# Graph-network kernel on one core: 64-wide products laid in pairs on the two column halves of TensorE, and the first message round reordered

## The chip, the cores and the metric

The kernel runs on one NeuronCore of a Trainium2 chip. The metric is the device time of one execution in microseconds (us). Three runs of the kernel before took 3177.02 to 3182.76 us, with a median of 3179.41 us. The engines are named as in the profile: PE is TensorE's matmul side and PEld its weight loads, DVE is VectorE, ACT is ScalarE, POOL is GpSimd, and SP issues transfers.

## The reference

Sixteen graphs (batches) of 1024 nodes with 64 channels go through four layers. `x` is [16, 1024, 64], `adj` is [16, 1024, 1024] with about 1.6% of its entries and its diagonal not zero, all in float32. Cut to what matters:

```python
x = layernorm(x + (adj @ (x @ W0) + b0))                      # layer 0
a = drop(adj)              # two neighbours of a row with over 10 of them are dropped, in both directions
agg = 0.25*q25(x, a) + 0.5*q50(x, a) + 0.25*q75(x, a)         # quantiles over a node's neighbours, per channel
x = layernorm(x + relu((x + agg) @ W1 + b1) @ W2 + b2)        # layer 1 (times the node mask)
h = x @ We
for i in range(3):
    h = relu(adj @ (h @ Wl[i] + bl[i]))
x = layernorm(x + (h @ Wp + bp))                              # layer 2 (times the node mask)
t = adj @ x
x = layernorm(x + where(t > 0.5, 1, 0))                       # layer 3
```

## The kernel before, in words

The nodes of a graph are 8 tiles (`T`) of 128. `adj` is transposed on TensorE, block by block, since its products need it with the source node on the partitions. Every batch goes through these parts, each written as a Python generator:

- `words_of` (with `transposed` and `Layer0`): rows of `adj` are loaded (`load_row`, L417, two buffers), transposed (L439) and copied out by ScalarE (L441). DVE tests the entries (`nb`, L526), TensorE packs the tests into words (L536). `Layer0.feed` (L464) multiplies the transposed tile with x: for every tile eight products with a weight of 128 rows by 64 columns and 128 moving columns, summed over the eight source tiles into partitions 0 to 63 of a PSUM bank. `Layer0.end` transposes x itself into the lower 64 partitions of `ax` (L478, copies L480), and one product per tile with W0 stacked on an identity (L485) gives adj x W0 plus x, with the bias. A layernorm gives x1.
- `front` and `listing`: the words become lists of neighbours, mostly on DVE (L646 one-hot rows, L694 to L710 list steps), with products that permute rows (L651, L652). Their last product for the table, L575, must be done before the table of x1 rows is written to DRAM.
- `gathered`: POOL gathers neighbour rows by indirect transfers (L815) into one of four sort buffers. `masked`: ScalarE adds a mask to each gathered row (L868). `quantiles`: DVE runs sorting networks of minimum and maximum over the rows (L906), in five groups of tiles per batch. `summed`: ScalarE weighs the sorted rows (L932), TensorE adds them with an identity (L936), and ScalarE or DVE copies the sums.
- `back`: `to_nodes` brings the aggregates into node order, with one-hot rows `ones_at` (L974 and L975 on ScalarE; in the last batch two of three on DVE, L971) and products of three bfloat16 pieces (L979), adds x1 (L985) and copies two halves to `oT` (L988). Then come the W1 product (L1172), `residual` with W2 (L1141, and L1147 and L1149 on DVE), layernorm to x2; `to_channels` transposes x2 (L367, copies L369); the embedding (L1185, copies L1187); three rounds, each with a message (bias L324, products L1196, copies L1199) and an aggregation over the whole of `adj` (L1207, 128 by 128 weights with 512 moving columns, relu L1210); the projection (L1141), layernorm to x3; `aggregate` for layer 3 (L377, 128 by 64 weights, 512 moving columns, copies L380), transposition back (L1219), the comparison on DVE (L1222), and the last layernorm. Layernorm's lines are L390 to L411, with ScalarE's square at L396 and DVE's last product at L411.

`adj` transposed is kept in DRAM per batch (`adjd`) and loaded whole (4 MB) into one buffer `adjB` for `back`.

The order of the work on each engine is written by the end of the function: every part has a planned start on a common clock, and a queue takes the part with the least time next. A part's `yield 1.3` says how long its last step is planned to take, times a stretch per part (`WORDS / WORDS_STEPS`, `BACK / BACK_STEPS` and so on). The five groups have planned lengths of 192 us together, which is the planned period of a batch:

```python
LENGTHS = (50.06, 35, 54.5, 19.5, 33)
...
            add(start(q), quantiles(st, g), (start(q + 1) - start(q)) / (cost + 0.1))
```

No time is measured: each engine runs its instructions in the order so written, and waits for their inputs. The setup before it (constants, weights, biases, the node mask) is ordered by dependencies; `centred` takes the mean over channels out of weights and biases that feed a layernorm, and `bias16` holds the biases in three bfloat16 pieces, added by a product with ones (`add_bias`, L324).

In f32 one product is two matmul instructions, each with its own weight load. At the end `general` stands for batches in which the lists run over; its branch is not taken here.

Of the kernel before, what the change touches and what calls it, by code (L numbers as in the profile page):

```python
# [10 lines left out]
F32 = mybir.dt.float32  # L11
# [142 lines left out]
def kernel(  # L154
# [126 lines left out]
    nc.scalar.dma_start(w0_sb[:C, :], w0)  # L281
    nc.vector.tensor_copy(w0_sb[C:, :], ident[C:, C:])
    w1_sb = load("w1_sb", [C, H], w1)
    b1_sb = load("b1_sb", [H, 1], b1.unsqueeze(1))
    w2_sb = load("w2_sb", [H, C], w2)
    we_sb = load("we_sb", [C, H], we)
# [11 lines left out]
    for v, n in ((w0_sb, 2 * C), (w2_sb, H), (wp_sb, H)):  # L298
        centred(v, n)
# [21 lines left out]

    def add_bias(bank, first, n, times):

        nc.tensor.matmul(bank[:, :times * n], ones16,  # L324
                         bias16[:, first:first + n].unsqueeze(1).to_broadcast([S, times, n]),
                         start=True, stop=False)
# [4 lines left out]
    mask_f = const.tile([B * T, P], F32, name="mask_f")  # L331
# [29 lines left out]

    def to_channels(dst, src):

        for h in range(NH):
            pt = psum_mm()
            for i in range(TH):
                nc.tensor.transpose(pt[:C, i * P:(i + 1) * P], src[:, h * TH + i, :], ident)  # L367
            yield 1.5
            nc.scalar.copy(dst[:, h * HALF:(h + 1) * HALF], pt[:C, :])  # L369
            yield 1.0  # L370

    def aggregate(dst, adjT, src, bank):

        for h in range(NH):
            pa = bank()
            for m in range(T):
                nc.tensor.matmul(pa[:C, :], src[:, m, :], adjT[:, h * TH:(h + 1) * TH, m, :],  # L377
                                 start=(m == 0), stop=(m == T - 1))
                yield 1.3
            nc.scalar.copy(dst[:, h * HALF:(h + 1) * HALF], pa[:C, :])  # L380
            yield 0.7
# [38 lines left out]
    def load_x(b):  # L420
        xt = act.tile([P, T + 1, C], F32, tag="x", name="xt")
        nc.vector.memset(xt[:, 0, :], 0.0)
        nc.sync.dma_start(xt[:, 1:, :], one(x, b).rearrange("o (t p) c -> p (o t) c", p=P))
# [28 lines left out]
    class Layer0:  # L452
# [6 lines left out]
        def feed(self, t, at):  # L459
# [3 lines left out]
            for m in range(T):  # L463
                nc.tensor.matmul(self.bank[:C, cols], self.xt[:, m + 1, :], at[:, m, :],  # L464
                                 start=(m == 0), stop=(m == T - 1))
            yield 2.4
            if t % TH == TH - 1:
                h = t // TH
                nc.scalar.copy(self.ax[:C, h * HALF:(h + 1) * HALF], self.bank[:C, :])
                yield 0.7  # L470

        def end(self, y):
            for h in range(NH):
                pt = psum_tp()
                for i in range(TH):

# [839 lines left out]
```

## Time and profile before

| What | us |
|---|---|
| Median of three runs | 3179.41 |
| Profiled execution: its span, the only time the page gives of it | 4328.2 |
| DVE busy in it | 2822.0 (65%) |
| PE busy | 2647.8 (61%) |
| PEld busy | 1635.7 (38%) |
| POOL busy | 2160.8 (50%) |
| ACT busy | 1914.0 (44%) |
| First and last sort step on DVE (L906) | from 266.8 to 4195.2 |
| Mean granted TensorE clock | 0.764 |

The profiled execution is 1149 us longer than the median of the runs. Shares of the span are therefore not shares of a timed run, while busy times of single instructions can be carried over. The largest groups on TensorE are L1207 (769.6 us in 1536 instructions), L936 (376.0 us), L464 (284.5 us in 1920), L377 (272.6 us in 512) and L979 (213.0 us in 768). DVE's largest groups are the forms of L906. A mean duration on PE mixes two clocks: the granted clock moves between half and full speed.

### The profile page before, as it was taken

Reading aid. Unit: us, or ns where it says so; the run is one execution under the profiler, and the core shown is the slowest. Engines: PE = TensorE matmul, PEld = TensorE weight load, DVE = VectorE, ACT = ScalarE, POOL = GpSimd, SP = SyncE. Lnnn points to the kernel's source line nnn. Section 1 sums busy time; section 2 is a strip of 40 time slices with the busy share of each in tenths; the row PEclk is TensorE's granted clock in tenths of the full one; section 3 lists DMA queues with packets and bytes.
Section 4 is the critical chain, followed back from the end, with each engine's and each line's share of the span. In section 5 each row is a group of like instructions: output and inputs, shape, how many; then the busy total and the mean of one; then the engine's idle time right before and its main releaser. Section 6 shows DMA issues by size and latency. Waiting matters only on the chain.

```text
span 4328.2 us, 46055 instructions
## 1 busy us (share of the span) xinstructions
PE 2647.8 (61%) x13765; PEld 1635.7 (38%) x13766; DVE 2822.0 (65%) x6935; ACT 1914.0 (44%) x6153; POOL 2160.8 (50%) x2078
## 2 busy tenths in 40 slices
PE   6034285675848567584755758476575848456478
PEld 5023152443525244352533435253343525233243
DVE  6058383865849486594857668485766859476671
ACT  2034352634536264453535455363545536253641
POOL 1715626455454645546465464546545554645600
PEclk8566597787969778796877879687787969768688
DMA  3212121322222132222213222231322222111210
GB/s 107 42 50 70 34 67 37 104 54 78 73 71 84 40 101 56 78 77 74 77 39 90 64 83 76 65 84 40 100 60 79 78 80 71 39 57 24 62 43 3
DMA packets 169056, 282.54 MB, mean 65 GB/s; under 512 B 99485, under 2 KB 102112, under 8 KB 166880
## 3 DMA queue, kind: packets, MB, share of 16 engines
q1 hardware_dynamic: 67584, 142.01, 9.9%
q0 software_dynamic: 66048, 69.88, 9.1%
q10 hardware_dynamic: 35168, 67.62, 4.1%
q8 instruction: 114, 1.87, 0.2%
q14 instruction: 142, 1.16, 0.1%
HBM read 204.33 MB, written 71.44 MB: 64 GB/s over the span
## 4 chain that ended last, share of the span: by engine, by line
another core or an unknown queue 28%; DVE 25%; PE 23%; ACT 16%; issue 7%; DMA 0%; ACTq 0%; DVEq 0%
DVE g L906 7%; PE mm L1207 7%; DVE s L906 7%; ACT g L868 6%; ACT ones_at L974 3%; PE ax L464 3%; ACT ones_at L975 2%; PE tp L439 2%; PE mm L377 2%; PE pa L936 2%; PE mm L1196 2%; ACT g L932 1%; PE mm L1141 1%; DVE top L707 1%
## 5 line engine op out<-in xcount | busy, mean ns | idle before, releaser
L815 POOL DMA_INDIRECT g<-table,idx x1952 | 2045.4, 1048 | 1919.7 <-PE pa L936 666.8
L1207 PE MATMUL mm<-adjB,msg 128*128 128x512 f32 x1536 | 769.6, 621 | 109.1 <-issue 82.4
L936 PE MATMUL pa<-g,ident 128*128 128x128 f32 (+1 forms) x1600 | 376.0, 360 | 430.1 <-ACT g L932 300.5
L868 ACT ACTIVATE g<-g,bias 128x64 f32<-128x64 f32 (+9 forms) x2272 | 596.8, 341 | 47.9 <-DVE bias L864 29.2
L906 DVE TENSOR_TENSOR s<-g 128x256 f32<-128x256 f32 (+9 forms) x944 | 531.3, 588 | 64.5 <-ACT g L868 55.5
L936 PEld LDWEIGHTS pa<-g,ident 128*128 128x128 f32 x1600 | 312.3, 248 | 574.0 <-ACT g L932 347.1
L906 DVE TENSOR_TENSOR g<-s 128x256 f32<-128x256 f32 (+8 forms) x864 | 473.4, 573 | 9.0 <-DVE s L906 3.0
L932 ACT ACTIVATE g<-g,w 128x64 f32<-128x64 f32 x1552 | 397.8, 341 | 17.2 <-DVE w L912 13.6
L1207 PEld LDWEIGHTS mm<-adjB,msg 128*128 128x128 f32 x1536 | 268.7, 197 | 301.1 <-issue 270.7
L1147 DVE TENSOR_TENSOR u<-mm,mb 128x512 f32<-128x512 f32 x32 | 22.1, 691 | 463.1 <-remote 313.5
L464 PE MATMUL ax<-at,xt 128*64 128x128 f32 x1920 | 284.5, 310 | 17.4 <-issue 17.4
L377 PE MATMUL mm<-adjB,x 128*64 128x512 f32 x512 | 272.6, 666 | 36.3 <-issue 31.3
L979 PE MATMUL mm<-ones_at,pieces 128*64 128x512 bf16 x768 | 213.0, 420 | 119.0 <-ACT ones_at L975 77.1
L464 PEld LDWEIGHTS ax<-at,xt 128*64 128x64 f32 x1920 | 250.2, 158 | 81.2 <-issue 79.1
L439 PE MATMUL tp<-ident,arow 128*128 128x128 f32 x1024 | 181.7, 309 | 156.2 <-remote 66.4
L399 DVE TENSOR_REDUCE ln_v<-sq 128x8 f32<-128x512 f32 x64 | 43.6, 681 | 296.4 <-issue 156.8
L439 PEld LDWEIGHTS tp<-ident,arow 128*128 128x128 f32 x1024 | 140.9, 162 | 205.1 <-issue 131.7
L441 ACT COPY at<-tp 128x512 f32<-128x512 f32 x240 | 139.0, 580 | 177.2 <-remote 122.3
L906 DVE TENSOR_TENSOR g<-g,s 128x256 f32<-128x256 f32 (+5 forms) x432 | 199.1, 464 | 15.1 <-remote 5.0
L906 DVE TENSOR_TENSOR g<-g 128x256 f32<-128x256 f32 (+8 forms) x304 | 200.7, 660 | 11.2 <-remote 4.0
L1219 PE MATMUL mm<-ident,tT 64*128 64x64 f32 x128 | 25.7, 295 | 293.9 <-ACT tT L380 207.4
L1210 ACT ACTIVATE hlT<-mm 128x512 f32<-128x512 f32 x96 | 57.4, 598 | 296.4 <-PE mm L1207 123.7
(225 smaller groups left out, 4361.9 us busy)
## 6 DMA issues: line engine op xcount, KB each, us to landing
arow<-in_adj_dram SPq DMA_DIRECT2D x128, 512.0 KB
adjd<-at ACTq DMA_DIRECT2D x120, 512.0 KB
adjB<-adjd SPq DMA_DIRECT2D x15, 4096.0 KB
g<-table,idx POOLq DMA_INDIRECT x1952
table<-xc ACTq DMA_DIRECT2D x16, 264.0 KB
xt<-in_x_dram SPq DMA_DIRECT2D x16, 256.0 KB
out_dram<-y SPq DMA_DIRECT2D x16, 256.0 KB
stage<-table,packed POOLq DMA_INDIRECT x112
```

The costliest lines, as they stand in the source:

```text
L377: nc.tensor.matmul(pa[:C, :], src[:, m, :], adjT[:, h * TH:(h + 1) * TH, m, :], start=(m == 0), stop=(m == T - 1))
L439: nc.tensor.transpose(pt[:, i * P:(i + 1) * P], a[:, j * P:(j + 1) * P], ident)
L441: nc.scalar.copy(at[:, h * TH:(h + 1) * TH, :], pt.rearrange("p (i n) -> p i n", n=P))
L464: nc.tensor.matmul(self.bank[:C, cols], self.xt[:, m + 1, :], at[:, m, :], start=(m == 0), stop=(m == T - 1))
L815: nc.gpsimd.indirect_dma_start(out=dst, out_offset=None, in_=st["table"], in_offset=bass.IndirectOffsetOnAxis(ap=index, axis=0))
L868: nc.scalar.activation(v, v, AF.Identity, bias=bias[:m, i, k:k + 1])
L906: nc.vector.tensor_tensor(box(bufs[mode >> 1 & 1], d, run, sd, count), box(bufs[mode >> 3], a, run, sa, count), box(bufs[mode >> 2 & 1], b ...
L932: nc.scalar.activation(slots(g, bufs[0], lo + r, lo + r + 1)[:, i, 0, :C], slots(g, bufs[at[r]], lo + r, lo + r + 1)[:, i, 0, :C], AF.Iden ...
L936: nc.tensor.matmul(pa[:, :(e - k) * nt * C], ident, rows_.rearrange("p (k c) -> p k c", c=R)[:, :, :C], start=(j == 0), stop=(j == len(run ...
L974: nc.scalar.activation(ones_at, iota, AF.Abs, bias=st["minus"][:, s:s + 1])
L979: nc.tensor.matmul(bank[:C, :], pieces[:, i, s, :], ones_at[:, h * HALF:(h + 1) * HALF], start=(s == 0 and i == 0), stop=False)
L1207: nc.tensor.matmul(pg, msg[:, m, :], adjT[:, h * TH:(h + 1) * TH, m, :], start=(m == 0), stop=(m == T - 1))
```

## The change

All 64-wide products of the main path that had the left half of the columns alone are laid in pairs, one on columns 0 to 63 and one on columns 64 to 127, which write partitions 0 to 63 and 64 to 127 of the same PSUM bank:

- `aggregate` and `to_nodes`: the two products of a pair have the same weights and different moving columns (two halves of the nodes). Their result is one [128, 512] tile with the first half of the nodes in the upper 64 partitions and the second in the lower, copied out once. `oT` and `tT` have this form, and so the W1 weight is held twice (once per half). `aggregate` for layer 3 pairs even and odd tiles, so that one 128 by 128 transposition brings back two tiles.
- `Layer0.feed`: even and odd source tiles go to different column halves. The two partial sums in `ax` are added by the next product, with W0 stacked twice. x itself is transposed into a tile of its own, and added by a second product per tile with a 0/1 weight (`self_sb`).
- `to_channels`, used on the branch for lists that run over, is paired likewise, with products in place of transpositions.

The first message round is reordered. Before: x2 is transposed, multiplied by We, then by Wl[0] with bias, then by `adj`. Now: `adj` times (x2 + 1), 64 wide, and then one product with a merged weight of We Wl[0]. We is centred, so that the added one and the mean of x2 give nothing through it, and the bias bl[0] divided by 64 is added to every row of the merged weight, so that the added one gives the bias. The merged weight is made in the setup (two column halves, each with a product of the bias pieces and one of We with Wl[0]).

`load_x` loses its tile of zeros and its memset. Planned step times are changed where the steps are. `mask_f`, `we_sb` and some setup tiles share buffers with tiles of the main part.

```diff
     w0_sb = const.tile([2 * C, C], F32, name="w0_sb")
-    nc.scalar.dma_start(w0_sb[:C, :], w0)
-    nc.vector.tensor_copy(w0_sb[C:, :], ident[C:, C:])
-    w1_sb = load("w1_sb", [C, H], w1)
+    self_sb = const.tile([2 * C, 2, C], F32, name="self_sb")
+    nc.vector.memset(self_sb, 0.0)
+    w1_sb = const.tile([2 * C, H], F32, name="w1_sb")
+    for h in range(2):
+        half = slice(h * C, (h + 1) * C)
+        nc.scalar.dma_start(w0_sb[half, :], w0)
+        nc.vector.tensor_copy(self_sb[half, h, :], ident[half, half])
+        nc.scalar.dma_start(w1_sb[half, :], w1)
...
+    weT = act.tile([H, C], F32, tag="x3", name="weT")
+    pe = ps.tile([P, HALF], F32, tag="mm", name="pe", bufs=2)
+    nc.tensor.transpose(pe[:, :C], we_sb, ident[:C, :C])
+    nc.vector.tensor_copy(weT, pe[:, :C])
+    centred(weT, H)
+    share16 = act.tile([S, P], BF16, tag="u", name="share16")
+    nc.vector.memset(share16, 1.0 / C)
+    wel_sb = const.tile([2 * C, H], F32, name="wel_sb")
+    pe = ps.tile([P, HALF], F32, tag="mm", name="pe", bufs=2)
+    for h in range(2):
+        half = slice(h * C, (h + 1) * C)
+        nc.tensor.matmul(pe[half, :H], share16[:, half], bias16[:, 3 * C:3 * C + H],
+                         start=True, stop=False)
+        nc.tensor.matmul(pe[half, :H], weT, wl_sb[:, 0, :], start=False, stop=True)
+    nc.vector.tensor_copy(wel_sb, pe[:, :H])
...
+    def rows_of(t, h):
+        return t[h * C:(h + 1) * C]
...
-    def aggregate(dst, adjT, src, bank):
-        for h in range(NH):
-            pa = bank()
-            for m in range(T):
-                nc.tensor.matmul(pa[:C, :], src[:, m, :], adjT[:, h * TH:(h + 1) * TH, m, :],
+    def aggregate(dst, adjT, src, bank, tiles):
+        pa = bank()
+        for m in range(T):
+            for h in range(NH):
+                nc.tensor.matmul(rows_of(pa, h), src[:, m, :], adjT[:, tiles[h], m, :],
                                  start=(m == 0), stop=(m == T - 1))
-                yield 1.3
-            nc.scalar.copy(dst[:, h * HALF:(h + 1) * HALF], pa[:C, :])
-            yield 0.7
+            yield 1.3
+        nc.scalar.copy(dst, pa)
+        yield 0.7
...
             for m in range(T):
-                nc.tensor.matmul(self.bank[:C, cols], self.xt[:, m + 1, :], at[:, m, :],
-                                 start=(m == 0), stop=(m == T - 1))
-            yield 2.4
+                nc.tensor.matmul(rows_of(self.bank, m % 2)[:, cols], self.xt[:, m, :], at[:, m, :],
+                                 start=(m < 2), stop=(m >= T - 2))
+            yield 1.6
...
             for t in range(T):
-                nc.tensor.matmul(pz[:, t * C:(t + 1) * C], self.ax[:, t * P:(t + 1) * P], w0_sb,
+                pzt = pz[:, t * C:(t + 1) * C]
+                nc.tensor.matmul(pzt, self.ax[:, t * P:(t + 1) * P], w0_sb, start=False, stop=False)
+                nc.tensor.matmul(pzt, xT[:, t // 2 * P:(t // 2 + 1) * P], self_sb[:, t % 2],
                                  start=False, stop=(t == T - 1))
...
-            for h, bank in enumerate(banks):
-                for i in range(S):
-                    nc.tensor.matmul(bank[:C, :], pieces[:, i, s, :],
+            for i in range(S):
+                for h in range(NH):
+                    nc.tensor.matmul(rows_of(bank, h), pieces[:, i, s, :],
                                      ones_at[:, h * HALF:(h + 1) * HALF],
                                      start=(s == 0 and i == 0), stop=False)
...
-        x2T = chan("x2T")
-        yield from to_channels(x2T, x2)
+        x2p = act.tile([P, T, C], F32, tag="msg", name="x2p")
+        nc.scalar.activation(x2p, x2, AF.Identity, bias=ones)
+        yield 1.0
+        gT = chan("gT")
+        yield from aggregate(gT, adjT, x2p, psum_mm,
+                             [slice(h * TH, (h + 1) * TH) for h in range(NH)])
         hT = act.tile([H, N], F32, tag="hT", name="h0T")
         for h in range(NH):
-            cols = slice(h * HALF, (h + 1) * HALF)
             ph = psum_mm()
-            nc.tensor.matmul(ph, we_sb, x2T[:, cols], start=True, stop=True)
+            nc.tensor.matmul(ph, rows_of(wel_sb, h), rows_of(gT, h), start=True, stop=True)
             yield 1.3
-            nc.scalar.copy(hT[:, cols], ph)
+            nc.scalar.activation(hT[:, h * HALF:(h + 1) * HALF], ph, AF.Relu)
             yield 0.7
-        for l in range(NL):
+        for l in range(1, NL):
...
-        yield from aggregate(tT, adjT, x3, psum_mm)
+        yield from aggregate(tT, adjT, x3, psum_mm, [slice(h, T, NH) for h in range(NH)])
```

## The prediction

> **What bounds the kernel now.** I read the page's head and the shares of the chain first, then the busy time by stretch, then the order of time on TensorE at the end and at the start.
>
> ```profile
> span 4328.2 us, 46055 instructions
> PE 2647.8 (61%) x13765; PEld 1635.7 (38%) x13766; DVE 2822.0 (65%) x6935; ACT 1914.0 (44%) x6153; POOL 2160.8 (50%) x2078
> ...
> another core or an unknown queue 28%; DVE 25%; PE 23%; ACT 16%; issue 7%; DMA 0%; ACTq 0%; DVEq 0%
> ```
>
> The profiled execution took 4328 us, 1149 us more than the median of the runs, 3179.4 us. [...] The chain has 28% under "another core or an unknown queue" and 7% under "issue", 35% or 1515 us: more than the whole excess. So the next view asks what the engines do in such a place. Columns are the stretch, its length, busy time and instructions of PE, PEld, DVE, ACT and POOL, then the granted clock.
>
> ```profile
> 1836.00:1944.00 108.00, 91.52 (x478) 58.14 (x478) 100.32 (x232) 57.86 (x208) 46.89 (x44) 0.92 0.27 76
> 2451.70:2484.20 32.50, 7.54 (x30) 6.52 (x31) 0.04 (x1) 5.55 (x22) 20.81 (x22) 0.55 0.18 40
> 266.80:4195.20 3928.40, 2459.69 (x12692) 1512.10 (x12691) 2727.26 (x6611) 1844.83 (x5983) 2053.64 (x1954) 0.77 0.24 66
> 4195.20:4328.20 133.00, 101.29 (x318) 49.96 (x318) 18.13 (x43) 28.47 (x53) 0.00 (x0) 0.81 0.10 36
> ```
>
> In the second row every engine but POOL nearly stands still, with no releaser that the trace names; I take such places to be the excess over a timed run. In the first row, which has none, VectorE (DVE) is busy 100.3 of 108 us, and the rest is its small gaps. That is the sorting stage at its own speed: DVE sets it, not TensorE. The count agrees. Sorting runs from 266.8 to 4195.2 us here and needs 2727 us of DVE, at 93% about 2930 us; the end after the last sort is 133 us; a head of about 150 us (gathers start at 96 us; the first group's 34, at the 1.25 us of one start to the next on POOL, take 43 us, and masking follows) makes 3210 us, already above 3179. So in timed runs DVE hardly waits between first and last sort; an estimate of its idle time there is 0 to 60 us. What the change can shorten for certain is where DVE stands: the end, and the head.
>
> **The end.** TensorE in order of time (start, length, instructions):
>
> ```profile
> 4207.04 6.48 PE L979 MATMUL mm<-ones_at,pieces 128*64 128x512 bf16 x18 [6.10 <-ACT ones_at L975]
> ...
> 4222.22 1.91 PE L985 MATMUL mm<-ident,xc 128*64 128x128 f32 x16
> ...
> 4233.08 1.92 PE L367 MATMUL mm<-ident,x 128*64 128x128 f32 x8 [4.79 <-DVE x L411]
> 4234.92 3.78 PE L1185 MATMUL mm<-x2T,we_sb 64*128 64x512 f32 x4
> ...
> 4243.57 15.17 PE L1207 MATMUL mm<-adjB,msg 128*128 128x512 f32 x32
> ...
> 4261.39 13.90 PE L1207 MATMUL mm<-adjB,msg 128*128 128x512 f32 x32
> ...
> 4298.87 16.55 PE L377 MATMUL mm<-adjB,x 128*64 128x512 f32 x32 [4.79 <-DVE x L411]
> ```
>
> An f32 product is two instructions of 0.43 us at full clock (13.9/32), 0.86 at half. L377, 64 wide, costs the same as L1207, 128 wide: half the columns idle.
>
> Do two 64-wide products on separate columns overlap? No row shows it, so bounds: 1.0 (serial) to 2.0 times the rate. [...] But L1207's 32 instructions, each with its own load over the same rows, fit in 13.9 us: the loads are hidden already. [...]
>
> Last L377: TensorE starts cold, about 5.6 us at half clock in the old one (6.5 instructions). Paired, those 5.6 us do 11.8 instructions; 20.2 are left at 0.43/1.8 = 0.24: 4.8 us. So 10.4 instead of 16.55: **-6.1 us**. The fourfold wide transposition after it replaces eight narrow ones, 0.5 us: even.
>
> First round: from x2 at 4233.0 to the end of L1207 at 4258.7 is 25.7 us. Removed: transposition L367 with two copies, embedding L1185, message L1196 with bias and copies, and one round. Added: adding one on ScalarE 0.8 (an activation of this size, L396, takes 0.63 and its start), paired aggregation 10.4, one copy 0.7, four instructions of the merged product 1.7: 13.6. **-12.1 us**.
>
> to_nodes: 48 products from the first ones_at at 4207.0 to 4222.2, 15.2 us. Paired, a step of six needs 0.8 instead of 1.4 us, and the one-hot rows then pace it (2.2 us on ScalarE for steps 0, 3, 6, 0.5 on DVE for the others, two buffers): about 9.7. **-5.5 us**. L985 halves, -0.9; its one copy lets the w1 product start later, +0.5. End together: **-24 us**.
>
> **The head.**
>
> ```profile
> 15.12 0.62 PE L536 MATMUL tp<-pow,nb 128*128 128x65 f16 x8
> 15.93 1.60 PE L439 MATMUL tp<-ident,arow 128*128 128x128 f32 x8 [0.18 <-ACT adjB L441]
> ...
> 21.88 1.06 PE L439 MATMUL tp<-ident,arow 128*128 128x128 f32 x8 [1.06 <-DMA arow<-in_adj_dram]
> ```
>
> The merged weight is made in the setup. In the built order its bias product stands on TensorE ahead of the first L536 and the third tile's L439, and it needs bias16, which DVE finishes at about 26 us now with three tiles' tests between, and at about 21 with them behind. Behind it stand mask, mask copy and then the first test, so the first L536 moves from 15.1 to about 24 and the third tile from 15.9 to about 25. Later rows of adj load only when a transposition frees one of two buffers (15.9 plus its 1 us, then 4.9 us to 21.88), so the eighth tile slips about as far, less a catch-up: **+8 us**. Two more weight loads and the moved one are queued ahead of the bias loads on ScalarE's queue, about 0.5 us each; they are inside this estimate. Given back: batch 0's Layer0 products (L464, 7.2 us twice) pair up, so the second half of the words no longer waits 1.25 us (DVE at 65.27, for ScalarE), and the product of L575, behind a 3.56 us L464 group, comes 1.6 us earlier. Net **+5 us**.
>
> **Between.** Per batch TensorE loses about 13.8/1.8 of two aggregations, half of L464 and L979, some 30 us; ScalarE drops seven copies of 0.58 us. I cost this at nothing: DVE's 176 us per batch cover it. Without that cover it would be worth up to the 60 us of idle time. The final products of Layer0 grow by 16 instructions (2.0 us as L485's), also under DVE. DVE itself loses one memset per batch (0.11 us at 14.0), about **-2 us**. New wait: ScalarE's x+1 waits for DVE's L411, with the g maskings and sums (L868, L932) behind it; before, TensorE waited there and ScalarE's copy behind it. The next sort waits for those maskings, but is planned a group ahead.
>
> Sum: 3179.4 - 24 + 5 - 2 = **3158 us** (-0.7%); in the profile's own terms 4328 - 21 = 4307, if its stalls stay as they are.
>
> **Rivals.** *DVE's idle time goes too.* POOL waits 667 us for L936, whose sums stand behind these products on TensorE; lighter, it frees gather buffers earlier. For it: 0 to 60 us of possible idle time; against: the stall-free stretch shows none. Half of 60: 3128.
>
> *The pairs run one after the other.* The plan's step times were cut: an aggregation now has 11.1 planned us, at 181 real (3179 - 150 - 133 over 16) to 192 planned per batch 10.3 us, and serial it takes 13.8 plus what other work stands between. DVE's L1222 comes right after and stops all sorts behind it by 3.5 to 7 us a batch, say 4 times 15 = 60; the end gains only about 6, the head loses 13. 3179 + 60 - 6 + 13 - 2 = 3244. It decides where the pair factor falls under 13.8/10.3 = 1.3. [...]
>
> *Paired, but the moved steps collide.* Everything of words_of and back is now placed earlier among the sorts; a wait of 3 us per batch (15 x 3) eats the gain: 3200.
>
> *Nothing moves*: head and overlap eat the end's gain, 3179.
>
> **How the numbers follow.** Chances: forecast 0.48 (its own range 3138 to 3172, 0.02 of it within 0.2%), idle time gone too 0.16, nothing 0.09, serial 0.18, collision 0.09. 0.2%, 6 us, is about what a measurement of this kernel can tell from no change. Faster 0.46 + 0.16 = 0.62; same 0.02 + 0.09 = 0.11; slower 0.18 + 0.09 = 0.27. The range, 3112 to 3228, takes in the idle-time case but for its far end, the collision, and the serial case only where its wait is under 3 us a batch (3244 - 15 = 3229); it leaves out about 0.03 below and 0.15 above.
>
> **What would show it.** Right: in the last 100 us the 64-wide f32 instructions start about 0.24 us apart when warm, and the end after the last sort is about 109 us; the first L536 at about 24 us; stall-free stretches still at 100 of 108 us of DVE. Wrong: starts 0.43 us apart; L1222 or L1147 on DVE waiting for TensorE in stretches without a stall; a first sort that does not slip.

## The result, and the profile after

The changed kernel takes 3249.74 us (median of 4 runs, 3246.61 to 3256.17), beside 3179.95 us of the kernel before in the same comparison: a ratio of 1.022, with an interval of 1.0206 to 1.0235. It is 70 us slower. The forecast was 3158 us, faster, and the range ended at 3228.

The head of the page of the changed kernel:

```profile
span 3248.3 us, 45347 instructions
PE 2228.8 (69%) x13484; PEld 1417.7 (44%) x13485; DVE 2833.3 (87%) x6933; ACT 1854.2 (57%) x6041; POOL 2272.2 (70%) x2078
```

The span is that of a timed run: none of the long stalls of the earlier profile of before are in it. So the kernel before was profiled again (the first experiment below), to have a trace of the same kind:

```profile
span 3173.8 us, 46055 instructions
PE 2501.1 (79%) x13765; PEld 1557.0 (49%) x13766; DVE 2823.7 (89%) x6935; ACT 1900.1 (60%) x6153; POOL 2276.9 (72%) x2078
```

The two spans differ by 74.5 us. The busy time by stretch says where: first the stage from the first to the last sort step, then what follows it (columns: stretch, length, busy time and instructions of PE, PEld, DVE, ACT, POOL, granted clock, DMA share, GB/s). The kernel before:

```profile
139.40:3042.60 2903.20, 2315.63 (x12692) 1434.44 (x12691) 2729.12 (x6611) 1831.22 (x5983) 2242.54 (x2031) 0.88 0.33 90
3042.60:3173.80 131.20, 99.87 (x318) 49.48 (x318) 18.12 (x43) 28.41 (x53) 0.00 (x0) 0.83 0.10 37
```

The changed kernel:

```profile
143.60:3141.80 2998.20, 2082.91 (x12410) 1321.93 (x12409) 2737.45 (x6604) 1791.10 (x5883) 2238.86 (x2033) 0.75 0.30 89
3141.80:3248.30 106.50, 71.29 (x288) 34.67 (x288) 15.31 (x36) 24.14 (x45) 0.00 (x0) 0.82 0.01 4
```

The first sort is 4.2 us later, the sorting stage 95.0 us longer, and the end 24.7 us shorter: +74.5 us. TensorE has 233 us less to do in the sorting stage, yet the stage is longer, and the granted clock there fell from 0.88 to 0.75. What DVE waited for over the whole span (us in total, times, longest), in the changed kernel and then, for the same two lines of the source, in the kernel before:

```profile
DVE u L1175 <- PE mm L1169: 117.9, 16, 48.5
DVE ln_v L425 <- ACT sq L422: 72.5, 32, 6.9
```

```profile
DVE u L1147 <- PE mm L1141: 77.1, 4, 59.8
DVE ln_v L399 <- ACT sq L396: 6.6, 11, 1.1
```

The longest wait ahead of `u` (59.8 and 48.5 us) stands in the end, behind the last sort, and is no loss of the sorting stage.

Summed over the sorting stage alone, DVE's gaps of over 0.3 us are 175.7 us, against 86.4 in the kernel before. Ahead of layernorm's reduction (L425; L399 in the kernel before) they went from 2.0 to 63.4 us, ahead of the residual's product with the mask (`u`, L1175; L1147 in the kernel before) from 8.0 to 61.2. Ahead of the hits (L888; L862 in the kernel before), DVE's test of gathered rows that a masking needs, they fell from 39.9 to 21.0. The two new waits, 61.4 and 53.2 us, are more than the whole loss of the stage. They recur in each steady batch (about the fourth to the thirteenth of the 16), whose period is 191.1 us, with about 4 us apiece. The period of before was 182 to 185.

### The profile page after: what moved, and what is told of

It is laid out like the page before. It is cut to its first block, busy times and chain, and to the rows that moved or that the text cites. A ratio compares the mean times of both kernels' runs of the same rounds, so it can differ in the third digit from the quotient of the medians.

```text
span 3248.3 us, 45347 instructions
## 1 busy us (share of the span) xinstructions
PE 2228.8 (69%) x13484; PEld 1417.7 (44%) x13485; DVE 2833.3 (87%) x6933; ACT 1854.2 (57%) x6041; POOL 2272.2 (70%) x2078
## 4 chain that ended last, share of the span: by engine, by line
DVE 31%; POOL 27%; PE 17%; issue 10%; DMA 7%; ACT 7%; DVEq 0%; POOLq 0%; ACTq 0%; SPq 0%
POOL g L841 25%; DVE s L932 9%; DVE g L932 8%; PE mm L1238 6%; DMA g<-table,idx 5%; DVE top L733 3%; PE pa L962 2%; POOL stage L841 2%; DVE kw L736 2%; ACT ones_at L1000 2%; ACT g L894 1%; DMA table<-xc 1%; PE ax L489 1%; PE mm L1227 1%; ACT ones_at L1001 1%
## 5 line engine op out<-in xcount | busy, mean ns | idle before, releaser
L841 POOL DMA_INDIRECT g<-table,idx x1952 | 2143.0, 1098 | 794.9 <-issue 568.4
L962 PE MATMUL pa<-g,ident 128*128 128x128 f32 (+1 forms) x1600 | 420.4, 402 | 412.9 <-ACT g L958 402.0
L962 PEld LDWEIGHTS pa<-g,ident 128*128 128x128 f32 x1600 | 340.7, 279 | 574.1 <-ACT g L958 487.4
L1238 PE MATMUL mm<-adjB,msg 128*128 128x512 f32 x1024 | 507.7, 620 | 8.4 <-ACT msg L1230 8.4
L1238 PEld LDWEIGHTS mm<-adjB,msg 128*128 128x128 f32 x1024 | 182.8, 200 | 154.2 <-issue 136.9
L912 ACT ACTIVATE hat<-iota,npos 128x10 f32<-128x10 f16 (+2 forms) x384 | 114.0, 297 | 175.7 <-DVE npos L901 175.5
L677 PE MATMUL wd<-hi,perm 128*128 128x71 f16 x960 | 116.6, 239 | 82.2 <-DVE perm L672 82.2
L677 PEld LDWEIGHTS <-perm 128*128 128x128 f16 x960 | 98.2, 127 | 141.3 <-DVE perm L672 102.8
L489 PE MATMUL ax<-at,xt 128*64 128x128 f32 x1920 | 158.9, 318 | 0.0
L489 PEld LDWEIGHTS ax<-at,xt 128*64 128x64 f32 x1920 | 128.3, 161 | 62.9 <-issue 62.3
L932 DVE TENSOR_TENSOR s<-s,g 128x256 f32<-128x256 f32 (+4 forms) x400 | 148.9, 376 | 6.7
```

What stands on the lines that cost most here:

```text
L489: nc.tensor.matmul(rows_of(self.bank, m % 2)[:, cols], self.xt[:, m, :], at[:, m, :], start=(m < 2), stop=(m >= T - 2))
L677: nc.tensor.matmul(pw[:, :hn], ws, hi[:, t, :], start=False, stop=False)
L841: nc.gpsimd.indirect_dma_start(out=dst, out_offset=None, in_=st["table"], in_offset=bass.IndirectOffsetOnAxis(ap=index, axis=0))
L912: nc.scalar.activation(h, iota[:, lo:lo + kw], AF.Abs, bias=npos[:, i, s:s + 1])
L932: nc.vector.tensor_tensor(box(bufs[mode >> 1 & 1], d, run, sd, count), box(bufs[mode >> 3], a, run, sa, count), box(bufs[mode >> 2 & 1], b ...
L962: nc.tensor.matmul(pa[:, :(e - k) * nt * C], ident, rows_.rearrange("p (k c) -> p k c", c=R)[:, :, :C], start=(j == 0), stop=(j == len(run ...
```

## What stands ahead of the two waits

The wait ahead of L425, in one batch of the changed kernel (TensorE in order of time: start, length, instructions, and in brackets the idle time before them and its releaser):

```profile
1636.96 0.79 PE L962 MATMUL pa<-g,ident 128*128 128x128 f32 x2 [7.68 <-ACT g L958]
...
1638.22 0.69 PE L510 MATMUL ax<-w_sb,ax 128*128 128x64 f32 x2
1638.70 0.63 PE L511 MATMUL ax<-self_sb,xT 128*128 128x64 f32 x2
...
1647.23 0.63 PE L511 MATMUL ax<-self_sb,xT 128*128 128x64 f32 x2
```

TensorE stands idle for 7.68 us ahead of a sum that waits for ScalarE. Then come Layer0's final products, the old ones (L510) and the added ones (L511), 32 instructions instead of 16. Each next two start 0.43 us later, 0.21 us an instruction. From the first to the last start they take 9.2 us, with sums between, where the 16 of before, also with sums between, took 4.0. The granted clock is the difference in kind. Busy times in such a stretch, in the changed kernel and in the kernel before (columns as above):

```profile
1637.00:1648.00 11.00, 11.00 (x49) 10.34 (x50) 7.23 (x21) 4.60 (x20) 8.56 (x9) 0.50 0.24 52
```

```profile
1592.90:1597.00 4.10, 4.10 (x21) 2.34 (x20) 3.82 (x20) 3.97 (x16) 3.19 (x4) 1.00 0.15 26
```

Before, TensorE came to these products out of other work, with no idle time over 1.7 us in the 15 us ahead of them in any steady batch, and ran them at full clock. ScalarE's square and DVE's L425 come directly behind:

```profile
1648.53 0.69 DVE L425 TENSOR_REDUCE ln_v<-sq 128x8 f32<-128x512 f32 x1 [3.96 <-ACT sq L422]
```

The wait ahead of L1175 has another look. TensorE just before it, and the wait:

```profile
1600.38 1.09 PE L489 MATMUL ax<-at,xt 128*64 128x128 f32 x16
1601.41 1.98 PE L1238 MATMUL mm<-adjB,msg 128*128 128x512 f32 x4
...
1603.90 1.55 PE L1169 MATMUL mm<-wp_sb,hlT 128*128 128x64 f32 x12
...
1606.32 0.69 DVE L1175 TENSOR_TENSOR u<-mm,mb 128x512 f32<-128x512 f32 x1 [4.23 <-PE mm L1169]
```

Nothing here is slow or idle: the granted clock is full from 1585 us on, the last round, words_of's transpositions and Layer0's feed (L489) follow one another without a gap, and the projection is 4.2 us late all the same. From DVE's u of the first residual to that of the second, one batch of before has 104.5 us of DVE's work in the plan. TensorE's chain, from the end of the W2 product to the end of the projection, takes 103.8 us and starts 0.9 earlier, so 1.6 us were in hand (0.1 to 1.9 in the steady batches: the plan of before was tight). In the changed kernel DVE has 81.1 us of its own there, 23.4 less, since the planned steps of the first round were cut by 22.3 (38.8 to 16.1, times the stretch of 178/181). TensorE's chain takes 87.9, only 15.9 less, and starts 2.6 earlier: 2.6 + 81.1 - 87.9 = -4.2, the wait.

## The experiments

**The kernel before, once more.** No edit.

> The kernel before, profiled again, for a trace without the long stalls. Theory (DVE waits are new): its period per batch is about 10 us shorter than the changed kernel's 191.1 us, so 181 to 185 us, and per batch DVE shows neither the wait of 4.2 us ahead of its L1147 (the changed kernel's L1175) nor the wait of 4.0 us ahead of layernorm's reduction of Layer0 (L399). Rival (the waits were there already and something else grew): both waits stand here too at 3 us or more, and the period is shorter in another place.

3175.53 us in a single run, and the trace shown above. But for one of 6.7 us ahead of L1147 at 2912 us, neither wait is there at 3 us or more in the sorting stage; the theory holds.

**Each cause alone.** Three edits on the changed kernel. First, Layer0 as before:

```diff
-                nc.tensor.matmul(rows_of(self.bank, m % 2)[:, cols], self.xt[:, m, :], at[:, m, :],
-                                 start=(m < 2), stop=(m >= T - 2))
-            yield 1.6
+                nc.tensor.matmul(self.bank[:C, cols], self.xt[:, m + 1, :], at[:, m, :],
+                                 start=(m == 0), stop=(m == T - 1))
+            yield 2.4
...
-                nc.tensor.matmul(pzt, xT[:, t // 2 * P:(t // 2 + 1) * P], self_sb[:, t % 2],
```

> The changed kernel with Layer0 alone as it was before: x transposed into the lower half of ax, unpaired products in feed, W0 stacked on an identity, the planned steps of this part as before. Theory: the 16 added products of Layer0's end, run at half clock (0.21 us each, 3.4 us), cause DVE's wait of 4.0 us ahead of L425 in each batch; the wait goes and 15 x 4.0 = 60 us with it: about 3190 us, between 3180 and 3215. The wait ahead of L1175 stays at about 4 us. Rival (another engine, POOL or TensorE, holds the period at 191 us and DVE's waits are only its slack): 3240 to 3255, with the idle time of DVE moved to another place.

Second, every product as changed, but with the old planned places of back's steps:

```diff
                 nc.tensor.matmul(rows_of(pa, h), src[:, m, :], adjT[:, tiles[h], m, :],
...
-            yield 1.3
+            yield 2.6
         nc.scalar.copy(dst, pa)
-        yield 0.7
+        yield 1.4
...
         nc.scalar.activation(x2p, x2, AF.Identity, bias=ones)
-        yield 1.0
+        yield 12.6
```

and 2.4 instead of 1.5 ahead of the copy in to_nodes.

> The changed kernel with every product as changed, but with the planned step times of back's parts set so that each later step of back has the planned place that it had before (aggregations 22.2 instead of 11.1 us, 11.6 us more ahead of the first one, to_nodes 0.9 more). Theory: back's last steps were planned some 35 us earlier, into a stretch where TensorE is full with words_of's transpositions, and so the second residual's product is late for DVE's L1175; with the old places that wait of 4.2 us per batch goes: 15 x 4.2 = 63 us, about 3187 us, between 3180 and 3215; the wait ahead of L425 stays at about 4 us. Rival (it is the amount or kind of work on TensorE that is late, not the place): 3235 to 3255 with the wait in place.

Third, the added product with half as many instructions:

```diff
-                nc.tensor.matmul(pzt, xT[:, t // 2 * P:(t // 2 + 1) * P], self_sb[:, t % 2],
-                                 start=False, stop=(t == T - 1))
                 if t % 2:
+                    nc.tensor.matmul(pz[:, (t - 1) * C:(t + 1) * C], xT[:, t // 2 * P:(t // 2 + 1) * P],
+                                     self_sb.rearrange("p a c -> p (a c)"),
+                                     start=False, stop=(t == T - 1))
                     yield 0.7
```

> The changed kernel with Layer0's self product laid as four products of 128 columns per batch with the two 0/1 weights side by side, instead of eight of 64 columns: 8 added instructions instead of 16. Theory: the wait ahead of L425 falls by about 8 x 0.21 = 1.7 us of 4.0, 15 x 1.7 = 25 us: 3224 us, between 3215 and 3235. Rival (the wait is set by the product L962 that stands ahead, or by the cold clock alone, not by the number of instructions): 3245 to 3252 with the wait still at 3.5 us or more.

| Run | us | ratio to before, interval | gaps ahead of L425 | ahead of L1175 |
|---|---|---|---|---|
| changed kernel | 3249.7 | 1.022 (1.0206 to 1.0235) | 63.4 | 61.2 |
| Layer0 as before | 3209.2 | 1.0103 (1.0086 to 1.0120) | 7.6 | 58.0 |
| old places of back's steps | 3180.5 | 1.0014 (1.0006 to 1.0023) | 39.8 | 11.6 |
| self product 128 wide | 3211.3 | 1.0112 (1.0095 to 1.0129) | 23.6 | 58.0 |

(Gaps: DVE's, over 0.3 us, in us over the sorting stage. Lines are named by the changed kernel's numbers here and below, also where a run's own differ by some.) The two edits of Layer0 leave the wait ahead of L1175 as it was. The old places take that wait and, against the expectation, a third of the other (63.4 to 39.8); why is told under the clock. Taking Layer0 back undoes more than the added products: they also stand elsewhere among the sums then. Halving the added instructions took 38 us, more than the expected 25: the wait fell from 3.97 to 0.92 us a batch, and the products' stretch from 9.2 to 6.3 us, so more than 8 x 0.21 = 1.7. In that run the later ones of them start 0.1 to 0.15 us apart: the granted clock came back from half to full among them, about 6 us after TensorE took up work again. That pointed at the clock.

**Do they add up?** Combinations on the changed kernel, with one more edit: the merged weight is made by a step of its own, planned at the start of the second group's sort, and not in the setup.

```diff
+    def merged():
+        weT = act.tile([H, C], F32, tag="x3", name="weT")
...
+        nc.vector.tensor_copy(wel_sb, pe[:, :H])
+    add(start(1), merged())
```

> Both of the earlier edits on the changed kernel: back's later steps at their old planned places, and the self product as four products of 128 columns. Theory (two separate waits of DVE that add up): what is left ahead of L425 in the run with the old places, 40 us, falls by about 25 to 30; the wait ahead of L1175 stays gone: 3150 to 3158 us, 20 to 25 us under the kernel before. Rival (the two edits remove the same time, since removing one lets DVE run into the next late engine, POOL's gathers above all): 3172 to 3185, with waits ahead of the maskings' hits grown by 20 us or more.

> As the run with both edits, and the merged weight is made not in the setup but beside the second group's sort, long before back needs it. Theory: the first packed test on TensorE and the third tile no longer stand behind it, and the first sort starts 3 to 6 us earlier, so the time is 3 to 5 us under that run: 3146 to 3154. Rival (the first sort is set by DVE or the loads of adj, not by TensorE's order): the same within 2 us.

> The changed kernel with Layer0 as before and back's later steps at their old planned places: the paired aggregations, paired to_nodes and the reordered round alone. Theory: neither of the two waits, so the end's gain of 25 us remains, less the head's 4 to 6: 3150 to 3158 us. Rival (paired products in back cost DVE something else in the sorting stage, for instance by the slower clock that a less busy TensorE is granted): 3165 to 3185.

> The run without the Layer0 part and with back's later steps at their old places, and the merged weight made beside the second group's sort and not in the setup. Theory (the setup's order delays the first sort by 10 us, as the pair of runs with and without it showed): 3155 less 8 to 12 us: 3143 to 3148 us, 1% under the kernel before. Rival (the 11 us between those two runs came from elsewhere, since their medians are of few runs): 3153 to 3157.

| Run | us | ratio, interval | first sort at |
|---|---|---|---|
| old places, self product 128 wide | 3175.4 | 0.9999 (0.9990 to 1.0007) | 144.6 |
| the same, merged weight late | 3164.7 | 0.9960 (0.9946 to 0.9974) | 134.4 |
| old places, Layer0 as before | 3155.3 | 0.9939 (0.9922 to 0.9955) | 146.0 |
| the same, merged weight late | 3150.4 | 0.9917 (0.9901 to 0.9934) | 137.6 |

The third row is what the forecast had described: paired aggregations, paired to_nodes and the reordered round, without a wait. It lies 20 us under before; its sorting stage is 2896.8 us against 2903.2 of before. With the old places, Layer0's part still costs 25 us (3180.5 against 3155.3), and with the new ones 41. The first row missed its expectation by 20 us: the two edits together took 5 us more than the old places alone. The time is the rival's, but not its mechanism, since the gaps ahead of the hits grew by 4 us only (32.6 to 36.4). Those ahead of L425 fell by less than reckoned, 39.8 to 27.8: in this run Layer0's products meet a mean clock of 0.55 in every steady batch and DVE waits 1.0 us each time, where with the old places alone every second batch had the full clock and no wait.

The setup's order costs what it was said to. The head of the last run (TensorE in order of time):

```profile
15.09 0.62 PE L546 MATMUL tp<-pow,nb 128*128 128x65 f16 x8
```

and that of the changed kernel, in which the merged weight's product waits for DVE's bias16:

```profile
21.97 0.26 PE L339 MATMUL pe<-bias,share 3*64 3x128 bf16 x1 [7.70 <-DVE bias L323]
...
25.56 0.62 PE L562 MATMUL tp<-pow,nb 128*128 128x65 f16 x8 [1.45 <-DVE nb L553]
26.00 1.95 PE L464 MATMUL tp<-ident,arow 128*128 128x128 f32 x8
```

With the weight made late the first sort starts 7 to 10 us earlier and the time is 4 to 11 us less, in three pairs of runs (the third is below). The fourth row lies between its two expectations, and is the fastest kernel of the study, 0.8% faster than before.

**The place, or the length of the plan?** Two single numbers on the changed kernel: all of back planned 24 us later (`AFTER` 25.2 instead of 1.2), and 6.5 planned us more between the two residuals (`yield 7.5` instead of 1.0 behind x+1).

> The changed kernel with one number changed: all of back is planned 24 us later (its start after the last group at 25.2 instead of 1.2 us), so that the second residual comes at its old place while every product and step time is as changed. Theory (the place against words_of's transpositions makes L1169 late): DVE's wait ahead of L1175 goes, 45 to 60 us: 3185 to 3205 us, with the wait ahead of L425 still there at 40 to 63 us. Rival (the wait follows the second residual wherever it is put, since the steps ahead of it are planned too short): 3235 to 3255.

> The changed kernel with one yield changed: 7.5 instead of 1.0 planned us behind the x+1, so that the stretch from the first residual to the second is planned 6.5 us longer. Theory: between the two residuals DVE is given 81 us of its own work, and TensorE needs 85 to 88 us (the trace: 87.8 from the end of the W2 product to the end of the projection, where the kernel before had 103.8 for 104.5 of DVE); the planned time fell by 22 us and TensorE's by 16, so 6.5 us more is enough: the wait ahead of L1175 falls from 61 us in all to under 10, and the time to 3185 to 3200. Rival (it takes the old place of all later steps, as in the run of the plan, since words_of's work moves against them): the wait stays at 30 us or more, 3215 to 3250.

The shift gave 3403.9 us (1.0717, 1.0699 to 1.0735), which no theory had expected. The gaps ahead of L1175 did fall to 25.9 us, but 123.1 us stand ahead of L425, where Layer0's products now take 13.2 us, and 82.2 ahead of DVE's addition of the sums (L975). Moving everything is no repair: other meetings come about. The 6.5 us gave 3190.3 us (1.0048, 1.0031 to 1.0065), as expected in time but not by the expected way. The wait ahead of L1175 went to 29.0 us with 31.5 new ones ahead of L1253, together as much as before; the time gained is that of the other wait, ahead of L425, which fell from 63.4 to 7.9. So a longer planned stretch moves the second wait, but this run does not show that it takes it away: with more time TensorE is also given more of words_of's work in it (its chain grew from 87.9 to between 91 and 93 us).

**The clock.** Products of zeros, which change nothing in the result, were put into TensorE's idle 7.7 us ahead of Layer0's last products:

```diff
                 nc.tensor.transpose(pt[:, i * P:(i + 1) * P], two, ident)
+            pz = psum_ax()
+            for _ in range(20 if self.warm else 0):
+                nc.tensor.matmul(pz, zeros, iota[:, :HALF], start=True, stop=True)
```

> The changed kernel with 20 products of zeros (f16, 128 columns by 512) put behind x's transposition in Layer0's end, into the bank that the next product starts anew: they fill the 7.7 us in which TensorE stands idle before Layer0's last products. Theory (those products run at half clock, 0.21 us each, because TensorE stood idle, and that makes the wait ahead of L425): they run at 0.11 us, the 32 of them and the sums between take some 5 us less, the wait falls from 63 us in all to under 15, and the time by 45 to 60 us: 3190 to 3205. Rival (the clock stays at half there whatever TensorE does, or the products behind are late for another reason): 3235 to 3260.

> As the run with 20 products of zeros, with 35: the 20 took 4.5 us at full clock and left TensorE idle for 3.35 us ahead of L962, and Layer0's last products came at half clock again, so that run told nothing of the cause. 35 take 7.4 us and leave under 1 us. Theory (the half clock makes the products late): L510 and L511 run at 0.11 us an instruction, the wait ahead of L425 falls from 63 us in all to under 15 and the time to 3190 to 3210 us. Rival (the clock stays at half, or ScalarE's sums between the products pace them): 3235 to 3260 with the wait in place.

> The kernel with 35 products of zeros ahead of Layer0's last products, once more. Theory (the half clock makes the products late): L510 and L511 run at 0.11 us an instruction, the wait ahead of L425 falls from 63 us in all to under 15 and the time to 3190 to 3210 us. Rival (the clock stays at half there, or ScalarE's sums between the products pace them): 3235 to 3260 with the wait in place.

With 20: 3249.5 us (1.0233, 1.0216 to 1.0251), nothing gained. TensorE in that run:

```profile
1628.07 4.48 PE L504 MATMUL ax<-iota,wide_ident 128*128 128x512 f16 x20
1635.90 0.80 PE L965 MATMUL pa<-g,ident 128*128 128x128 f32 x2 [3.35 <-ACT g L961]
...
1637.64 0.63 PE L513 MATMUL ax<-self_sb,xT 128*128 128x64 f32 x2
```

The zeros started 0.216 us apart, faster than reckoned, and left 3.35 us idle. Layer0's products behind that ran at half clock again, 0.21 us an instruction, in every steady batch. A first run with 35 took 4557.2 us where the kernel before took 4361.8 in the same comparison. Its trace has long stalls of all engines, as the first profile of before has, so it says nothing on the wait. A second one, beside 3176.8 us of before: 3171.9 us (0.9990, 0.9979 to 1.0001). TensorE in this run:

```profile
1590.45 7.72 PE L504 MATMUL ax<-iota,wide_ident 128*128 128x512 f16 x35
...
1598.75 0.43 PE L512 MATMUL ax<-w_sb,ax 128*128 128x64 f32 x2
1599.03 0.39 PE L513 MATMUL ax<-self_sb,xT 128*128 128x64 f32 x2
```

The same 32 instructions now take 0.11 us each and 4.8 us from the first to the last start, half of 9.2. The sorting stage is 2912.5 us. The gaps ahead of L425 fell from 63.4 to 8.3 us, and, what was not expected, those ahead of L1175 from 61.2 to 29.3: TensorE's chain between the residuals now starts 4.0 us ahead of DVE's u instead of 2.6 and takes 86.8 us instead of 87.9. 525 useless products made the kernel 78 us faster. So the half clock is shown to be the cause of the first wait. That the zeros took half of the second as well is measured; by which way is not shown.

The run with the old places holds the same experiment in itself: from the eighth batch on, Layer0's products take 9.2 us in every second batch, and DVE waits 3.4 us ahead of L425 in those; in the others they take 4.8, with no wait there over 0.3 us. One batch of each kind (columns as above):

```profile
1600.00:1609.40 9.40, 9.40 (x45) 9.31 (x44) 5.91 (x18) 4.08 (x17) 7.27 (x8) 0.50 0.17 28
1785.30:1790.20 4.90, 4.90 (x45) 4.87 (x44) 4.65 (x14) 4.25 (x17) 3.73 (x4) 1.00 0.17 31
```

In both kinds TensorE stood idle for the same 1.75 us just before.

**The causes together.** The last three runs put the repairs together.

> The changed kernel with Layer0 as before, 6.5 more planned us behind the x+1, and the merged weight made beside the second group's sort. Theory (the two waits were two causes and each repair takes its own): 3190 of the run with 6.5 us, less 41 for Layer0 and 5 to 8 for the setup's order: 3141 to 3150 us. Rival (with both gone DVE catches up with TensorE's chain between the residuals, and 6.5 us are too few): 3155 to 3175 with 30 us or more of waits ahead of the u of L1175 or L1253.

> The changed kernel with 35 products of zeros ahead of Layer0's last products and the merged weight made beside the second group's sort. Theory: the first sort starts some 10 us earlier (147 to 137 us) and the time falls from 3172 by as much: 3160 to 3165 us, with 25 to 30 us of waits ahead of L1175 left. Rival (the earlier start is lost again to POOL or the clock): 3168 to 3175.

> As that, with back's later steps at their old planned places too. Theory (planned places and half clock are separate): the 25 to 30 us ahead of L1175 go: 3135 to 3148 us, the fastest of all. Rival (at the old places other products meet, as the run with 6.5 us and Layer0 as before showed that repairs don't add up; or POOL's gathers, 180 us per batch, take over): 3152 to 3175.

6.5 us more, Layer0 as before, weight late: 3244.0 us (1.0211, 1.0190 to 1.0231), against an expectation of 3141 to 3150, with 80.3 us of gaps ahead of u in the residuals and 51.2 ahead of L1253's. The rival's form of it came true, but larger: TensorE's chain between the residuals takes 95.4 us in most batches, of which the unpaired feed has 12 to 13, against 91 to 93 and about 8 with the paired one. Zeros with the weight late: 3168.0 us (0.9982, 0.9975 to 0.9989), 4 us less than without and at the edge of the rival's range; the first sort came 7 us earlier. All with the old places: 3228.3 us (1.0170, 1.0153 to 1.0187), against an expectation of under 3148. The trace says why:

```profile
1798.84 1.10 PE L1158 MATMUL mm<-wp_sb,hlT 128*128 128x64 f32 x8
...
1800.23 7.72 PE L490 MATMUL ax<-iota,wide_ident 128*128 128x512 f16 x35
1807.78 1.00 PE L1158 MATMUL mm<-wp_sb,hlT 128*128 128x64 f32 x8
```

At the old places Layer0's end meets the projection. The zeros, made for an idle stretch, stand for 7.7 us in the middle of it, and DVE's u waits 5 to 8 us in each steady batch (104.3 us of gaps in all).

**A grid under all of them.** The traces show one thing more. The granted clock changes on a grid of 3.41 us: the 235 stretches between two changes in the trace of the changed kernel, and the 197 in the first trace of before, are whole multiples of 3.4133 us, to 1 ns. The period of a steady batch is a whole multiple too in most of the runs in which DVE waits for TensorE in every batch. It is 191.1 us, or 56.0 steps, in the changed kernel, in the run with 20 zeros, and in the one with 6.5 us more, Layer0 as before and the weight late. It is 55.0 steps with Layer0 as before and with the self product 128 wide; 54.0 with the 35 zeros (weight in the setup or late) and with old places and self product together; and 59.0 with the shift. With the old places two periods make 108.0 steps, with old places and zeros together 111.0, and with 6.5 us alone five make 272.0. The kernel before (53.6) and the fastest two runs, in which DVE seldom waits for TensorE, keep to no whole number. If the grid holds the period, taking a wait away shows in steps of 3.41 us a batch, some 50 us in all, and not in the size of what was taken: Layer0 as before and the self product 128 wide left 7.6 and 23.6 us ahead of L425, and their times differ by 2 us. That the clock's grid holds the period fast is an inference from this agreement; no run was made to test it.

## Why the prediction was wrong, by its own steps

- **The pair factor held, and was taken too low.** 1.8 was taken, a guess between the bounds of 1.0 and 2.0. No run shows that term; what the runs show in its place is 2.0. In the last layer-3 aggregation at full clock the two instructions of a pair start 3 to 4 ns apart and the next pair 0.43 us later, as single instructions did before: a factor of 2.0, 0.21 us an instruction where 0.24 was named. It took 9.10 us (10.4 forecast, 15.92 in the clean trace of before). Feed's sixteen take 1.09 us instead of 1.96. The row of L1207 was the right one to read for the weight loads: the 32 instructions of the paired aggregation have 32 loads of their own and still keep this distance, so no load stands open.

TensorE at the end, in the changed kernel, and then the last aggregation in the clean trace of before:

```profile
3152.18 3.67 PE L1005 MATMUL mm<-ones_at,pieces 128*64 128x512 bf16 x18 [6.09 <-ACT ones_at L1001]
...
3173.86 9.73 PE L403 MATMUL mm<-adjB,x2p 128*64 128x512 f32 x32 [5.54 <-ACT x2p L1208]
...
3226.33 9.10 PE L403 MATMUL mm<-adjB,x 128*64 128x512 f32 x32 [4.79 <-DVE x L437]
```

```profile
3145.07 15.92 PE L377 MATMUL mm<-adjB,x 128*64 128x512 f32 x32 [4.79 <-DVE x L411]
```

- **The end held.** -24 forecast, -24.7 measured (131.2 to 106.5). The first round from x2 is 12.4 us after and 24.5 before, -12.1 as forecast; to_nodes 10.2 and 15.3, -5.1 for -5.5; the last aggregation -6.8 for -6.1.
- **The head held.** +5 forecast, +4.2 between the two traces; the first L562 at 25.6 us and the third tile at 26.0, for 24 and 25.
- **"Between ... I cost this at nothing: DVE's 176 us per batch cover it" failed.** It is the step that turns the sign: +95 us, where the memset alone was to give -2. DVE's own busy time in the stage is 8 us longer, not 2 shorter, spread thinly over many lines; for that I have no cause. The rest is waits, with two terms:
  - *"The final products of Layer0 grow by 16 instructions (2.0 us as L485's), also under DVE."* The duration was carried over from a row in which TensorE was warm, that is, at full clock (2.0 us from 65.98 us, granted 1.00). Here it had been idle for 7.7 us, and the added stretch was 5.2 us, not 2.0. At full clock, with the 35 zeros, it was 0.8 (4.8 for 4.0): 2.0 was not too little, and what was wrong is the clock. The idle time came with the new places of back's steps; with the old ones it is 1.75 us. DVE did not cover the stretch, because L425 follows it through ScalarE with no work in hand. The cost of this part, by taking it out, is 41 us. Half clock stood behind an idle time of 7.7 us in the changed kernel, of 3.35 us in every steady batch of the run with 20 zeros, and of 1.75 us in every second batch of the run with the old places. At the 0.21 us an instruction of such a stretch the 16 added ones come to 3.4 us, as an estimate. The clock did not come back in some 12 us of TensorE's work without a gap (0.50 from 1636.96 to 1649 us).
  - The planned step times were compared with the real ones for the layer-3 aggregation only, in the serial rival, and there the test was the right one: what the plan takes from DVE's side against what TensorE really gives back. For the first round it would have read 22.3 planned against 12 (at the end, with nothing between) to 16 (between the sorts) real.
- **The estimate of 0 to 60 us of idle time in the stage of before** was too small, 86 us in gaps of over 0.3 us; it did not decide.
- **Of the rivals, "paired, but the moved steps collide" was the mechanism**, with 3 us per batch where the two waits cost about 8, and a chance of 0.09. "DVE's L1147 waiting for TensorE", named as what would show the prediction wrong, is what was seen. The forecast's 30 us of TensorE time saved per batch would be 480 in all; busy time fell by 272. The products that the change left alone took 138 us more, half of it the sums (L936; L962 in the changed kernel), whose instructions took 350 ns before and 403 after, with the granted clock in the stage down from 0.88 to 0.75.

What stays open: why the repairs of the second wait don't add up in general. The runs show that the planned places, the zeros, and which of words_of's products fall into the stretch all move that wait, and the periods agree with the grid of 3.41 us, but that was not tested and no formula for the wait was found.

## What to carry to other kernels

In a kernel whose order is written from planned times, cutting a step's planned time moves work of every engine; compare for each stretch between two of the bound engine's waits what the plan takes from it and what the other engine truly gives back, and what was in hand before. A saving on TensorE where it is not the bound can lengthen the short chains on which the bound engine does wait. Here TensorE stood idle for 7.7 us ahead of such a chain where there had been 1.7 us at most in the clean trace of before, the granted clock behind it was 0.50 instead of 1.00, and 32 instructions took 9.2 us that take 4.8 at full clock: cost such chains at the half clock. Change the work and the plan in separate steps, since each alone may have the opposite sign of the sum.

## What the runs showed of the hardware

- TensorE under dense work stayed at half clock: in the changed kernel Layer0's products and the sums between them ran back to back from 1636.96 us for about 12 us at 0.21 us per 64-wide f32 instruction, without coming to full clock (granted clock 0.50 from 1633 to 1674 us). With the self product 128 wide, the clock rose after about 6 us of it (the pair of L512's instructions takes 0.74 us up to 1624.22 us and 0.44 at 1626.22, with work again from 1619.91).
- The granted clock changed on a grid of 3.41 us: all 235 stretches between two changes in the changed kernel's trace, and all 197 in the first one of before, are whole multiples of 3.4133 us, to 1 ns. An idle time of 1.75 us ahead of Layer0's products went with half clock in one batch and with full clock in the next (old places, 0.50 and 1.00).
- An f16 product of 128 columns by 512 with weights of its own took 0.22 us at full clock (35 in 7.72 us), and filling an idle stretch of 7.7 us with them kept the next products at full clock (32 in 4.8 us instead of 9.2).
- Two 64-wide f32 products on the two column halves ran at twice the rate of one after the other; both use all 128 rows and have weight loads of their own (32 loads for 32 instructions). The two started 3 to 4 ns apart and the next two 0.43 us later, the distance of single ones before (512 moving columns, full clock).
